# A convolution on one core: the steps that make later weights paced over the images, their loads a set earlier, and GpSimd released by an earlier VectorE step

## Chip, cores and metric

The kernel runs on one core of one Trainium2 chip. The metric is the time of one execution on the device in microseconds (us). Runs of the kernel before took 978.03, 979.94 and 983.44 us; their median, 979.94 us, is the time before.

## What is computed

The input has 160 images of 128 channels and 32 by 32 pixels. They belong to five sets of weights. In the kernel's order, an image has a place from 0 to 159, and 32 in a row use the same set.

```python
xn  = group_norm(x, groups=32)            # groups of 4 channels, eps 1e-5
s1  = (max(U) - min(U)) / 3;  s2 = s1 / 5
v1  = s1 * floor(U / s1);     v2 = s2 * floor((U - v1) / s2)
w   = (v1 + v2).reshape(5 * 128, 128, 3, 3)
out = x + conv3x3(xn, w, padding=1, groups=5)
```

The weights are quantised from `U` in two floors, and the result of the convolution is added to the input.

## The kernel before

**Tiling.** One image is one tile of 128 partitions (channels) by 1024 pixels, and two images make a chunk. The normalised image is held in two parts of 16 bits, a high one (`hi` or `vh`) and a low one (`lo` or `vl`), and TensorE multiplies both by the weights. A 3 by 3 convolution over a pair of lines or columns is done with fewer products than nine: sums and differences of neighbours are multiplied by sums and differences of the weights.

**Two kinds of image.** For some images only the low part goes through the sums (`rows`, made by `low_part` L697 and `combinations` L710 to L719). For the *combined* images (`combined`, from image 7 on every odd one; from image 126 on more than half) the sums are taken of the image itself: GpSimd writes the outer columns (`outer_columns`, L632) and one difference (L662) into `v`, VectorE writes the rest (`combine`, L644 and L651), ScalarE scales it to the high part `vh` (L684), and VectorE makes the low part `vl` (`low_combined`, L690).

**One pass of the loop**, for image i, writes instructions for several images in the order of each engine's queue:

- TensorE: the sums of image i+1 into the banks `m1a` or `m1b` and `m2`, then the main products of image i into its bank pair `eo` (L734, L789).
- VectorE: the low part of image i+2; then `pairs` (L846, L848), which turns the sums of image i+1 into the start of its bank pair `eo`; then `combine` for image i+4.
- GpSimd: the differences of image i+4, or its normalised form `z` (L668), together called `beside_pairs`; then the DMA that adds a finished result to its image in memory (L897). Every eight images also the power -0.5 of the variances (L247).
- ScalarE: the copy of a finished bank pair (L874), the copy `m` of the sums (L837), the high parts, and the two passes that measure image means and squares (L202, L209).
- SP (the queue of loads and stores): the load of a coming chunk (L455), and the store of a finished one (L902). The queue is in order. A load waits until the chunk whose buffer it takes has been stored.

Nothing is scheduled by a planner: the order is the order in which the Python code writes the instructions, and engines wait for one another by semaphores. The one wait added by hand is `after`: GpSimd's differences and its power step wait for the VectorE instruction `last`, the one that stands ahead of `pairs`, so that they run beside `pairs`.

**Weights of the later sets.** While images of set n run, VectorE makes the weights of set n+1: three columns with 14 steps each (L101 to L127, and L507), 42 in all, on tiles of 128 by 384. `load_set` (L448) loads the raw weights into the only buffer of its pool. Each column is transposed by TensorE and kept by ScalarE (L527). Then six more VectorE steps (`sums_of_set`, L531 to L533) make the tables of sums. All steps stand in a generator `later`, from which each pass takes one or more:

```python
if b == (2 if n == 0 else 0):
    self.load_set(n + 1)
if b == (4 if n == 0 else 2):
    later = (s for col in self.COLS for s in self.make_column(n + 1, col))
```

Here b is the image's place in its set. Two steps are taken between one `pairs` and the next: for image i+2 not combined, one between `lo` and `rows` and one ahead of `pairs`; else one right after the preceding `pairs` and one between `vl` and `pairs`. At b of 28 what is left of `later` is written at once.

The statistics of eight images make a group. After the power step, VectorE scales them (`scales_by_vector`, L268 and L270), at the end of the pass, behind `combine`.

Of the kernel before, what the change touches and what calls it, by code (L numbers as in the profile page):

```python
# [16 lines left out]
N_SETS = 5  # L17
# [11 lines left out]


WIDEST = 40.0


class Steps:
# [107 lines left out]
def run(steps):  # L142

    while True:
        try:
            next(steps)
        except StopIteration as end:
            return end.value
# [197 lines left out]
class Main:  # L346
# [308 lines left out]
    def beside_pairs(self, i, after):  # L655
# [14 lines left out]
            )  # L670
        self.after(ins, after)

    def after(self, ins, before):

        self.tc.add_manual_dep(
            ins.ins, before.ins.name,
            mybir.DependencyInfo(mybir.DependencyClass.Sync, mybir.DependencyReason.DATA),
            reason="beside_pairs",
        )
# [226 lines left out]
    def run(self):  # L906
# [49 lines left out]
        def take(steps, count, last=None):  # L956
            for _ in range(count):
                last = next(steps, None) or last
            return last
# [73 lines left out]
        run(self.combinations(3))  # L1033
        self.steps.choose()
        ready, middle, scaled, measured, loaded = [], [], [], self.EARLY, 6
        later, turned = iter(()), []
        for i in range(self.imgs):
            n, b = self.place(i)

# [31 lines left out]
            ahead = i + min(10 + i // 4, self.STAT_LEAD + 1)  # L1071
            to_measure = range(measured, min(self.imgs, ahead))
            measured += len(to_measure)
            if n + 1 < N_SETS:
                if b == (2 if n == 0 else 0):
                    self.load_set(n + 1)
                if b == (4 if n == 0 else 2):
                    later = (s for col in self.COLS for s in self.make_column(n + 1, col))
            by_scalar = [k for k in to_measure if not self.by_vector(k)]
            by_vector = [k for k in to_measure if self.by_vector(k)]  # L1080

            if i < self.FIRST:

                if i == 0:
                    measure(0, 8, 9, 10)
                    self.normalise(4)
                    self.high_part(4)
                if i == 2:
                    self.leave(3)
                    self.normalise(5)  # L1090
                    measure(1, 9)
                    self.high_part(5)
                    self.pairs(3)
                    measure(0, 11)
                    self.low_part(4)
                    run(self.combinations(4))
                self.residual(j)
            else:

                last = None  # L1100
                if self.combined(i + 2):
                    last = last_of(self.low_combined(i + 2))
                elif i + 2 < self.imgs:
                    self.low_part(i + 2)
                    take(later, 1)
                    last = last_of(self.combinations(i + 2))
                last = take(later, 1, last)
                for st in scaled:
                    self.after(st.power(), last)
                if i + 4 < self.imgs:  # L1110
                    self.beside_pairs(i + 4, last)
                if i > self.FIRST and self.by_hand(j):
                    self.residual(j)
                for k in by_scalar:
                    self.measure(k, (0,))
                if i > self.FIRST and not self.by_hand(j):
                    self.residual(j)
                    self.accumulate(j)
                part = i + 3 < self.imgs and not self.combined(i + 3)
                if i + 1 < self.imgs:  # L1120
                    self.leave(i + 1)
                for st in ready:
                    if not st.late:
                        st.deviations()
                if part:
                    if self.by_scalar_too(i + 3):
                        self.normalise(i + 3)
                    self.high_part(i + 3)
                if self.combined(i + 3):
                    self.high_combined(i + 3)  # L1130
                for k in by_scalar:
                    self.measure(k, (1,))
# [8 lines left out]
            for n_of, col in turned:  # L1141
                self.keep_taps(n_of, col)
                if col == self.COLS[-1]:
                    later = self.sums_of_set(n_of)
            turned = []

            if i >= self.FIRST:

                if i + 1 < self.imgs:
                    self.pairs(i + 1)  # L1150
                if self.combined(i + 4):
                    self.combine(i + 4)
                else:
                    take(later, 1)
                if b == self.per_set - 4:
                    run(later)
                for st in ready:
                    if st.late:
                        st.deviations_by_vector()
                for st in scaled:  # L1160
                    st.scales_by_vector()

            scaled, middle, ready = [st for st in middle if st.late], ready, []
            if i >= self.FIRST:
                measure(0, *by_vector)
# [57 lines left out]
```

## Time and profile before

| | us |
|---|---|
| median of 3 runs (lowest to highest) | 979.94 (978.03 to 983.44) |
| the profiled execution, its own time | 982.18 |
| its span | 980.5 |
| TensorE busy (matmuls) | 943.3 |
| VectorE busy | 913.8 |
| ScalarE busy | 833.4 |
| GpSimd busy | 353.5 |

The profile is of one execution. Its lines name the engine (PE is TensorE, PEld its weight loads, DVE is VectorE, ACT is ScalarE, POOL is GpSimd, SPq the queue of SP), the line of the code, the output and the inputs by the program's names without their numbers, and the shapes. In a timeline a line begins with the start and the duration in us; a bracket at its end tells how long the engine sat idle before it and what ended that.

### The profile page before, as it was taken

How to read it: one execution, taken by the hardware profiler on the slowest of the kernel's cores; microseconds unless marked ns; L12 is line 12 of the kernel's file. 1: busy time of each engine (PE TensorE's matmuls, PEld its weight loads, DVE VectorE, ACT ScalarE, POOL GpSimd, SP SyncE). 2: the span in 40 equal slices, each digit the busy share in tenths (PEclk: the TensorE clock that was granted, in tenths of full speed). 3: DMA queues.
4: the chain of work that ended last, by engine and by line, in shares of the span. 5: the costliest groups of instructions: out<-in, count | busy, mean ns of one | idle time of the engine just before them, and what ended most of it. 6: DMA issues, size and time to landing. Idle time of an engine off the chain costs nothing.

```text
span 980.5 us, 13236 instructions
## 1 busy us (share of the span) xinstructions
PE 943.3 (96%) x4504; PEld 440.8 (45%) x4504; DVE 913.8 (93%) x1332; ACT 833.4 (85%) x1135; POOL 353.5 (36%) x441
## 2 busy tenths in 40 slices
PE   2899999999999999999999999999999999999997
PEld 1444444444444444444444444444444444444443
DVE  7999999998999999899999998799999998989995
ACT  5779889999999999889898989698989899898551
POOL 4353333343333333333343333233433434333530
PEclk9999999999999999999999999999999999999999
DMA  9627889999998888999998999998989989998774
GB/s 352 264 95 207 230 236 267 265 250 257 319 297 242 269 232 244 257 289 273 250 267 240 272 247 253 285 281 265 239 261 259 258 249 269 247 247 251 178 207 160
DMA packets 65117, 245.86 MB, mean 251 GB/s; under 512 B 5008, under 2 KB 5008, under 8 KB 65040
## 3 DMA queue, kind: packets, MB, share of 16 engines
q1 hardware_dynamic: 45312, 173.09, 49.4%
q0 software_dynamic: 19728, 71.84, 38.8%
q8 instruction: 37, 0.61, 0.2%
q14 instruction: 40, 0.33, 0.1%
HBM read 89.19 MB, written 83.89 MB: 177 GB/s over the span
## 4 chain that ended last, share of the span: by engine, by line
PE 74%; DVE 12%; DMA 6%; issue 4%; ACT 2%; POOL 2%; SPq 0%; DVEq 0%; POOLq 0%
PE eo L789 25%; PE eo L734 23%; PE m L789 12%; PE m1b L789 8%; PE m1a L789 5%; DMA out_dram<-xt 3%; DVE vl L690 2%; DVE v L644 1%; DMA u<-in_L_conv_U_dram 1%; DVE lo L697 1%; DVE eo L846 1%; DMA xt<-sum 1%; DMA range<-in_L_conv_U_dram 1%; DVE eo L848 1%; DVE v L651 1%
## 5 line engine op out<-in xcount | busy, mean ns | idle before, releaser
L734 PE MATMUL eo<-hi,wt 128*128 128x496 f16 (+2 forms) x1386 | 367.7, 375 | 0.7 <-ACT wt L527 0.7
L789 PEld LDWEIGHTS <-wt 128*128 128x128 f16 x1884 | 183.9, 99 | 216.1 <-DVE rows L719 5.2
L734 PEld LDWEIGHTS <-wt 128*128 128x128 f16 x1458 | 142.6, 99 | 163.7 <-ACT wt L527 1.4
L874 ACT COPY sum<-eo 128x1024 f32<-128x1024 f32 x137 | 143.1, 1045 | 63.2 <-PE eo L789 63.0
L690 DVE SCALAR_TENSOR_TENSOR vl<-v,rstd,vh 128x2048 f16<-128x2048 f32 x82 | 192.2, 2344 | 1.4 <-ACT vh L684 1.4
L789 PE MATMUL eo<-vh,wt 128*128 128x496 f16 (+1 forms) x492 | 185.0, 376 | 1.0 <-DVE eo L848 0.9
L789 PE MATMUL eo<-vl,wt 128*128 128x496 f16 (+1 forms) x492 | 184.9, 376 | 0.0
L684 ACT ACTIVATE vh<-v,rstd 128x2048 f16<-128x2048 f32 x82 | 164.1, 2001 | 17.1 <-DVE v L651 16.9
L209 ACT ACTIVATE junk<-xt,mv 128x1024 f16<-128x1024 f32 x152 | 174.3, 1147 | 0.1
L202 ACT ACTIVATE junk<-xt 128x1024 f16<-128x1024 f32 x152 | 160.6, 1057 | 15.2 <-DMA xt<-in_x_dram 11.6
L789 PE MATMUL eo<-rows,wt 128*128 128x496 f16 (+1 forms) x450 | 170.8, 380 | 0.0
L789 PEld LDWEIGHTS <-across 128*128 128x128 f16 x984 | 96.2, 98 | 116.0 <-issue 5.1
L668 POOL TENSOR_SCALAR z<-xt,ngm,rstd 128x1024 f32<-128x1024 f32 x53 | 62.8, 1184 | 232.3 <-DVE tt L109 39.6
L632 POOL TENSOR_SCALAR v<-xt,ngm 128x64 f32<-128x64 f32 x82 | 30.9, 377 | 257.1 <-issue 72.7
L897 POOL DMA_DIRECT2D xt<-sum x137 | 119.8, 878 | 4.4 <-ACT sum L874 3.1
L837 ACT ACTIVATE m<-m 128x512 f32<-128x512 f32 x157 | 94.0, 599 | 24.9 <-PE m L789 18.7
L644 DVE TENSOR_TENSOR v<-xt 128x960 f32<-128x960 f32 x82 | 106.2, 1295 | 2.8 <-POOL v L632 2.8
L789 PE MATMUL m<-vl,across 128*128 128x496 f16 (+1 forms) x246 | 92.1, 374 | 3.3 <-DVE vl L690 3.2
L697 DVE TENSOR_TENSOR lo<-z,hi 128x1024 f16<-128x1024 f32 x78 | 94.9, 1216 | 0.0
L789 PE MATMUL m<-vh,across 128*128 128x496 f16 (+1 forms) x246 | 92.1, 375 | 0.0
L662 POOL TENSOR_TENSOR v<-xt 128x512 f32<-128x512 f32 x82 | 84.8, 1034 | 0.0
L602 ACT CAST hi<-z 128x1024 f16<-128x1024 f32 x78 | 81.5, 1044 | 1.2 <-POOL z L668 0.5
(144 smaller groups left out, 1151.8 us busy)
## 6 DMA issues: line engine op xcount, KB each, us to landing
xt<-in_x_dram SPq DMA_DIRECT2D x78, 1024.0 KB, 7.0
out_dram<-xt SPq DMA_DIRECT2D x78, 1024.0 KB, 8.7
xt<-sum POOLq DMA_DIRECT2D x137, 512.0 KB, 7.2
u<-in_L_conv_U_dram SPq DMA_DIRECT2D x4, 576.0 KB, 9.7
xt<-in_x_dram SPq DMA_DIRECT2D x4, 512.0 KB, 9.9
range<-in_L_conv_U_dram SPq DMA_DIRECT2D x3, 576.0 KB, 8.1
out_dram<-xt SPq DMA_DIRECT2D x3, 512.0 KB, 2.7
u<-in_L_conv_U_dram SPq DMA_DIRECT2D x2, 288.0 KB, 3.0
```

The lines of the kernel that those rows point to most:

```text
L202: self.nc.scalar.activation(junk, image, ACTF.Copy, scale=-1.0 / image.shape[1], accum_out=self.mv[:, j, 0:1],)
L209: self.nc.scalar.activation(junk, image, ACTF.Square, bias=self.mv[:, j, 0:1], accum_out=self.mv[:, j, 1:2],)
L644: nc.vector.tensor_tensor(self.view(v, 1, (511, 2), (half, H), (1, half - 1)), self.view(x, 1, (1, 2), (W, H), (2, half - 1)), self.view(x ...
L662: ins = nc.gpsimd.tensor_sub(self.v[i][:, 1536:], odd, even)
L684: self.nc.scalar.mul(vh, self.v[i], st.rstd[:, j])
L690: yield self.nc.vector.scalar_tensor_tensor(vl, self.v[i], st.rstd[:, j], self.hi[i], ALU.mult, ALU.subtract)
L697: self.nc.vector.tensor_sub(lo[:, 1 : self.H + 1, :].rearrange("p h w -> p (h w)"), self.z.pop(i), self.hi[i].rearrange("p h w -> p (h w)"),)
L734: nc.tensor.matmul(self.bank(target, a)[:, first:end, c0:c1], self.wts[n, col][:, k, :], tile[:, s0 : s0 + 2 * (end - first) - 1 : 2, c0 + ...
L789: self.nc.tensor.matmul(out, weights, moving, start=start and j == 0, stop=False, skip_group_check=True)
L837: self.nc.scalar.mul(m2, self.m2_ps, 0.5)
L874: nc.scalar.copy(self.as_banks(i, self.sum[i]), self.flat(i, eo))
L897: self.nc.gpsimd.dma_start(self.image(i), self.sum.pop(i), accum_op=ALU.add)
```

## The change

- `load_set(n + 2)` is called at b of 30, two images ahead of the end of a set: at image 30 for set 2, 62 for set 3 and 94 for set 4, instead of 32, 64 and 96. Set 1 is loaded at image 2, as before.
- The steps of a column start at b of 1 instead of 2 (set 0: 4, as before), and a class `Later` hands them out at a pace: an account grows by 42/25 with each image (set 0: 42/22), and each step takes 1 from it. The sums are handed out with a pace of 3 an image. What is left is written at b of 28 and again at b of 30.
- For a combined image i+2, up to two steps are written between `vl` and `pairs`; the step behind the preceding `pairs` is taken only where image i+4 is not combined and the account allows it.
- GpSimd's power step and differences depend on the VectorE instruction ahead of `last` (`last_but_one`).
- `scales_by_vector` is written right behind `pairs`, ahead of `combine`.

`SCALAR` and `take_scalar` of the new class are not used by the program.

```diff
+class Later:
+    def __init__(self, steps=(), pace=0.0):
+        self.steps = iter(steps)
+        self.pace, self.due = pace, 0.0
+        self.scalar = False
+    def next_image(self):
+        self.due += self.pace
+    def take(self, count, last=None):
+        for _ in range(count):
+            if not self.scalar and self.due >= 1.0:
+                step = next(self.steps, None)
+                self.scalar = step is SCALAR
+                if not self.scalar:
+                    last = step or last
+                    self.due -= 1.0
+        return last
...
+    def finish(self):
+        run(self.steps)
...
+    def last_but_one(self, last):
+        of_engine = (
+            i for i in reversed(self.nc.cur_bb.bb.instructions) if i.engine == last.ins.engine
+        )
+        next(of_engine)
+        return next(of_engine)
...
-        later, turned = iter(()), []
+        later, turned = Later(), []
...
+            if i == 2:
+                self.load_set(1)
+            if b == self.per_set - 2 and n + 2 < N_SETS:
+                self.load_set(n + 2)
             if n + 1 < N_SETS:
-                if b == (2 if n == 0 else 0):
-                    self.load_set(n + 1)
-                if b == (4 if n == 0 else 2):
-                    later = (s for col in self.COLS for s in self.make_column(n + 1, col))
+                if b == (4 if n == 0 else 1):
+                    later = Later(
+                        (s for col in self.COLS for s in self.make_column(n + 1, col)),
+                        42 / (self.per_set - 6 - b),
+                    )
+            later.next_image()
...
-                    take(later, 1)
+                    later.take(1)
                     last = last_of(self.combinations(i + 2))
-                last = take(later, 1, last)
-                for st in scaled:
-                    self.after(st.power(), last)
+                last = later.take(2 if self.combined(i + 2) else 1, last)
                 if i + 4 < self.imgs:
-                    self.beside_pairs(i + 4, last)
+                    before = self.last_but_one(last)
+                    for st in scaled:
+                        self.after(st.power(), before)
+                    self.beside_pairs(i + 4, before)
...
-                    later = self.sums_of_set(n_of)
+                    later = Later(self.sums_of_set(n_of), 3.0)
...
                     self.pairs(i + 1)
+                for st in scaled:
+                    st.scales_by_vector()
                 if self.combined(i + 4):
                     self.combine(i + 4)
                 else:
-                    take(later, 1)
-                if b == self.per_set - 4:
-                    run(later)
+                    later.take(1)
+                if b in (self.per_set - 4, self.per_set - 2):
+                    later.finish()
...
-                for st in scaled:
-                    st.scales_by_vector()
```

More of the change, by code (lines that the diff above doesn't have):

```diff
@@ L31, with take_scalar @@
 WIDEST = 40.0
+SCALAR = "the next step is ScalarE's"
+class Later:
[14 more added lines that the diff above has]
+        return last
+    def take_scalar(self):
+        if self.scalar:
+            next(self.steps)
+            self.scalar = False
+    def finish(self):
+        run(self.steps)
 class Steps:
@@ L671, in beside_pairs @@
         self.after(ins, after)
+    def last_but_one(self, last):
[4 more added lines that the diff above has]
+        return next(of_engine)
     def after(self, ins, before):
         self.tc.add_manual_dep(
-            ins.ins, before.ins.name,
+            ins.ins, before.name,
             mybir.DependencyInfo(mybir.DependencyClass.Sync, mybir.DependencyReason.DATA),
```

## Prediction

> **What bounds the kernel now.** I read the page's busy times first, then the stretches of 20 us, then the waits of TensorE, then the timeline where it waits.
>
> ```profile
> PE 943.3 (96%) x4504; PEld 440.8 (45%) x4504; DVE 913.8 (93%) x1332; ACT 833.4 (85%) x1135; POOL 353.5 (36%) x441
> 120.00:140.00 20.00, 18.23 (x88) 8.32 (x87) 19.79 (x35) 18.58 (x26) 4.21 (x5) 1.00 0.87 233
> 140.00:160.00 20.00, 18.01 (x86) 8.00 (x85) 19.54 (x31) 16.26 (x22) 6.35 (x8) 1.00 0.89 246
> 160.00:180.00 20.00, 19.43 (x96) 9.19 (x94) 19.79 (x31) 19.27 (x31) 10.89 (x16) 1.00 1.04 290
> ...
> 620.00:640.00 20.00, 17.80 (x80) 7.76 (x79) 13.95 (x26) 15.80 (x21) 4.20 (x5) 0.91 0.98 319
> ```
>
> The columns are the length, then busy us of PE, PEld, DVE, ACT and POOL, then TensorE's clock. Every stretch from 180 to 960 us but 620:640 shows 19.86 to 20.00 of PE, so TensorE sets the time there, however full VectorE is. PE's idle 37 us lie in the first 80 us (23.3), after 960 (6.7), and in the four rows above (6.5). Only these rows are within the change's reach.
>
> ```profile
> 124.38 0.39 PE L789 MATMUL eo<-vh,wt 128*128 128x512 f16 x1 [0.40 <-DVE eo L848]
> 128.78 0.38 PE L789 MATMUL m<-vl,across 128*128 128x512 f16 x1 [1.34 <-DVE vl L690]
> 148.36 0.82 PE L789 MATMUL m<-rows,wt 128*128 128x512 f16 x3 [0.37 <-DVE rows L719]
> 150.17 0.39 PE L789 MATMUL eo<-vh,wt 128*128 128x512 f16 x1 [0.34 <-DVE eo L848]
> 154.37 0.38 PE L789 MATMUL m<-vl,across 128*128 128x512 f16 x1 [1.27 <-DVE vl L690]
> 178.49 0.38 PE L789 MATMUL m<-vl,across 128*128 128x512 f16 x1 [0.56 <-DVE vl L690]
> ```
>
> Six waits, 4.28 us, all for VectorE, which is 98 to 99% busy in those rows: here VectorE is the bound. The other place is one event.
>
> ```profile
> 614.19 0.46 SPq L448 DMA_DIRECT2D u<-in_L_conv_U_dram  x1
> 626.17 0.47 DVE L101 TENSOR_SCALAR nnn<-u,s1r 128x384 int16<-128x384 f32 x1 [5.95 <-DMA u<-in_L_conv_U_dram]
> 627.98 0.82 PE L789 MATMUL m<-rows,wt 128*128 128x512 f16 x3 [2.01 <-DVE rows L719]
> 629.97 0.61 PE L789 MATMUL eo<-vh,wt 128*128 128x512 f16 x1 [0.19 <-DVE eo L848]
> ```
>
> The first step on the weights of the last set waits 5.95 us for them, VectorE's rows come late behind it, PE idles 2.20 us, and then its matmuls take 0.6 us instead of 0.38: the clock is at half for 3.41 us (mean 0.91 in the row), which costs another 1.7. Together 3.9 us. The other three later sets did not wait for their weights.
>
> **What the skill says.** "SBUF — State Buffer", section "SBUF: two separate sides": VectorE's instructions with two SBUF inputs and GpSimd's instructions exclude each other; whichever starts first keeps the shared port for its whole length. The trace agrees: L644 takes 1.15 us alone, about 1.31 in half of its 82 cases, where L662 of GpSimd still runs, and 1.99 in the five behind a power step.
>
> ```profile
> 140.94 1.03 POOL L247 TENSOR_TENSOR rstd<-ve,mhalf 128x4 f32<-128x4 f32 x1 [2.67 <-DVE tt L110]
> 141.98 0.37 POOL L632 TENSOR_SCALAR v<-xt,ngm 128x64 f32<-128x64 f32 x1
> 142.32 1.03 POOL L662 TENSOR_TENSOR v<-xt 128x512 f32<-128x512 f32 x1
> ...
> 142.39 1.99 DVE L644 TENSOR_TENSOR v<-xt 128x960 f32<-128x960 f32 x1 [0.26 <-POOL v L632]
> ```
>
> "TensorE: Matmul & The Clock Gate", "What's actually happening": after an idle window of about 3.4 us the array's clock is halved until it has been busy for one. Here 2.01 us of idleness sufficed for one window of 3.41 us. "VectorE: DVE Perf Modes", "The DRAIN you can't avoid": a semaphore between consecutive instructions costs nothing extra. The trace differs where the second needs the first's result: in a row, L109 to L112 start 0.65 us apart (35.93, 36.58, 37.24, 37.89), while between other work such a step takes some 0.53 us of VectorE's time. So 0.12 us for each such pair.
>
> **The change part by part.** The sum stands on the profiled execution, 982.18 us (span 980.5, and 1.7 around it), 2.2 above the median of 979.94; without the 3.9 us event it would be 978.3, next to the fastest run (978.03). I therefore take it that the event lies in some runs only. That is a choice, since the runs have no traces.
>
> 1. *Weights in the preceding set.* SP issues in order, and its loads wait for stores to land (69 waits, 568.2 us). Before, the load stood behind the pair at 613.26 and 613.72; the entry ahead of that is the store at 599.90, 13.4 us earlier. Image 30 puts it right behind that store, at some 600.3. With the same 12 us it lands at 612.3. The first step moves one image forward, to about 615.3 (pairs of image 98 start at 615.9). It is 3 us early instead of 6 late. For set 2 it is 227.4 plus 9.7, against a step at 245. Its buffer was last read some eight images earlier, so SP gains no wait. Behind it on SP stand an image load and a store; 576 KB at 250 GB/s delays these by 2.4 us at most. ScalarE would meet that (it waited 1.8 us for an image at 619.75) and has room (18.1 of 20 busy). Gain 3.9 in a run with the event, 0 otherwise.
>
> 2. *Pacing.* 42 steps at 42/22 an image in set 0 (42/25 later) instead of two. In the two programs' order, up to the vl step ahead of the waits at 128.78, 154.37 and 178.49, the changed one has 17, 24 and 32 steps where there were 19, 27 and 35. A step is worth 0.5: 1.0, 1.5 and 1.5 us. One of them is only moved behind the vl step, and GpSimd's start follows it. Against that, both steps of an image with combined parts now stand in a row: three, four and six dependent pairs, 0.4, 0.5 and 0.7 us. Net 0.6, 1.0, 0.8. The eo steps now come 2.5 us after vl (two steps and 1.34); TensorE's twelve products from vl to eo last 2.5 as well, so I add nothing.
>
> 3. *GpSimd one step earlier.* GpSimd starts 0.12 to 0.18 us after the VectorE step that it waits for. Released by the step before, it would stand at the port when the last one ends, and that delay is gone. L644's surplus from 66 us on is 0.09, 0.10, 0.11, 0.17, then 0.84 with a gap of 0.35, 0.15, and 0.84 with 0.35. Small ones vanish (0.5 by 128, 0.6 by 154); a power step saves 0.2 to 0.6, I take 0.4 for each of two. Bounds: 0, if GpSimd isn't ready at the port, and 0.2 us a pair of images. 0.9 by 128, 1.4 by 154, 1.6 by 178.
>
> 4. *Scales ahead of the combination.* L268 and L270 (0.3 us) now stand right behind the eo steps and can wait for the power: at most 1.67 less 1.34, and a landing, 0.45 us, once in eight images. Where the combination follows, VectorE waited there for L632 anyway. I take 0 for the stretch.
>
> 5. *Sums and the rest.* In sets 0 to 2 the sums come some three images later; at the end of set 3 six of 0.35 us now meet the denser combined images from 124 on. In the chain of waits vl takes 2.26 us of VectorE, the two v steps 1.21 and 0.66, the eo steps 1.34, lo 1.13 and rows 1.3: pairs 124 to 126 then need 18.0 us (6.9, 4.8 and 6.3), against the 17.3 between pairs 123 and 126 (766.6 to 783.9). VectorE has a lead there; 0 to 1.5, I take 0.3. Otherwise, between 180 and 960 us, PE is full, so fewer VectorE steps gain nothing.
>
> Waits left in the stretch: by 128, 1.74 less 1.5; by 154, 3.72 less 2.4, so 1.3; by 178, 4.28 less 2.4, so 1.9. Once waited, time is not gained back, so about 1.9 stays: gain 2.4 (1.0 to 4.0). Sum: 982.18 - 3.9 - 2.4 + 0.3 = 976.2.
>
> **The rivals.**
> - *The stretch clears wholly.* Power steps run beside the last step, and vl ahead of its step counts. Then 4.28 is gained: 982.2 - 8.2 = 974.0, a floor. For it: every wait there is VectorE's. Against it: the dependent pairs.
> - *The weights' event is not in the runs, or comes back.* If SP lags, or u lands in 15 us instead of 12, the step waits again: 976.2 + 3.9 = 980.1. With the stretch unchanged as well, 978 to 982.
> - *GpSimd takes the port from vl (slower).* Where no step is left, 23 times, the last VectorE step is vl itself (L690), and GpSimd is released by what stands ahead. If vl then waits for ScalarE by more than GpSimd's 0.15 us, L632 and L662 take the port for 1.42 us, or L668 for 1.18. All 23 times 1.4 is 32 us on VectorE; if a third reaches PE, 976.2 + 11 = 987. Against it: vl waited for vh three times, 1.4 us in all, and the set's ends and set 4 have VectorE at 16 to 19 of 20.
>
> **How the numbers follow.** A run can tell about 0.5% from no change, 4.9 us: faster is below 975.0, slower above 984.8. The likeliest, 976.2 (974.8 to 978), has 0.43, of which a tenth lies below 975.0; the cleared stretch 0.29, nearly all below; the event's return or nothing gained 0.14; the lost port 0.14. Faster 0.33, same 0.53, slower 0.14. The range starts at the floor less the runs' scatter, 973.5, and reaches to 982.5; 0.14 above and a few hundredths below are left out.
>
> **What would show it.** In the changed profile: no wait of L101 for u, and no half clock near 628 us; DVE waits of PE between 118 and 180 us down from 4.28 to about 1.9; L644 nearer 1.15 than its mean of 1.30; POOL's L632 starting within 0.05 us of the end of a VectorE step. Wrong if PE shows new waits past 180 us, if L690 is lengthened past 2.36 us, or if L644 stays at 1.3.

## The result and the profile after

The first four runs of the changed kernel took 992.05, 992.38, 994.58 and 995.92 us; four runs of the kernel before in the same batch took 978.03 to 983.44. The ratio was 1.0128 [1.0088, 1.0169], so these runs were slower by 1.3%, and the prediction, 976.2 us in a range of 973.5 to 982.5, missed. Later runs of the same kernel differ among themselves: of 62 runs on three chips (e5, e12 and f4 below) 24 took 974.5 to 976.7 us, and 28 took 985 to 1002.6. Both have to be explained.

Medians and counts below are over all runs of a kernel; a ratio compares only those runs that lie within 1.5% of the fastest of their kernel.

The profile is of the run of 994.58 us (span 992.9). I call it and its like a late run, since its images come late. First the page: the busy times, and the engines' shares of the chain of work that ended last.

```profile
PE 946.7 (95%) x4504; PEld 439.1 (44%) x4504; DVE 914.3 (92%) x1332; ACT 827.8 (83%) x1135; POOL 418.5 (42%) x441
...
PE 30%; DMA 24%; DVE 22%; issue 10%; ACT 8%; POOL 4%; SPq 0%; DVEq 0%; POOLq 0%; ACTq 0%
```

The same line of the chain in the profile before:

```profile
PE 74%; DVE 12%; DMA 6%; issue 4%; ACT 2%; POOL 2%; SPq 0%; DVEq 0%; POOLq 0%
```

No engine is busy for much longer except GpSimd (353.5 us before), and in the chain DMA has 24% where it had 6%. Next the part that the prediction spoke of, from 118 to 180 us: what TensorE waited for there, the first step on the last set's weights, and one combination behind a power step, all from the timeline.

```profile
123.23 0.39 PE L830 MATMUL eo<-vh,wt 128*128 128x512 f16 x1 [0.21 <-DVE eo L889]
127.16 0.38 PE L830 MATMUL m<-vl,across 128*128 128x512 f16 x1 [0.87 <-DVE vl L731]
136.56 0.39 PE L830 MATMUL eo<-vh,wt 128*128 128x512 f16 x1 [0.21 <-DVE eo L889]
138.91 1.07 POOL L280 TENSOR_TENSOR rstd<-ve,mhalf 128x4 f32<-128x4 f32 x1 [1.84 <-DVE vl L731]
141.50 1.15 DVE L677 TENSOR_TENSOR v<-xt 128x960 f32<-128x960 f32 x1
152.11 0.38 PE L830 MATMUL m<-vl,across 128*128 128x512 f16 x1 [1.01 <-DVE vl L731]
176.06 0.38 PE L830 MATMUL m<-vl,across 128*128 128x512 f16 x1 [0.23 <-DVE vl L731]
...
629.44 0.77 DVE L134 TENSOR_SCALAR nnn<-u,s1r 128x384 int16<-128x384 f32 x1 [0.98 <-DMA u<-in_L_conv_U_dram]
```

The waits are down from 4.28 to 2.53 us. The combination (L677, before it was L644) takes 1.15 us behind a power step, where it took 1.99. The first step on the weights of each of the three later sets waited for them (1.96, 3.06 and 0.98 us): they were asked for earlier, but took 15.5 to 17.4 us to land, where they took 9.4 to 12.0 in the profile before. By 226 us the changed kernel is 2.5 us ahead: the pairs of image 31 start at 226.1 instead of 228.6. All of the loss comes after that. One window of TensorE's busy time with the count of its matmuls shows it; for comparison the same window of the changed kernel in a later, undisturbed run of 975.5 us (e12, span 973.8) follows.

```profile
242.00:694.00 452.00, 439.24 (x2084) 202.07 (x2083) 413.64 (x602) 389.62 (x543) 174.54 (x179) 1.00 0.94 255
```

```profile
242.00:694.00 452.00, 452.00 (x2171) 212.07 (x2170) 434.01 (x628) 409.97 (x564) 180.87 (x186) 1.00 0.95 266
```

The second has 87 matmuls more in the same time; at 452.00 us for 2171 of them that is 18.1 us, of the 19.1 by which the spans differ. (Busy time differs by 12.8 us only; the ends of matmuls are modelled in a profile, so I go by the count.) The waits of the late run name the cause (columns: total us, times, longest).

```profile
ACT junk L235 <- DMA xt<-in_x_dram: 73.2, 29, 7.4
PE m L830 <- ACT m L878: 11.6, 12, 2.1
...
SPq L488 <- DMA out_dram<-xt: 698.5, 69, 15.2
SPq L943 <- DMA xt<-sum: 118.7, 28, 14.7
```

The first and the third of these in the profile before:

```profile
ACT junk L202 <- DMA xt<-in_x_dram: 11.6, 3, 8.1
SPq L455 <- DMA out_dram<-xt: 568.2, 69, 13.6
```

ScalarE waits 29 times for an image that has not arrived, where it waited 3 times. The pass that measures an image (L235) is ahead of the copy `m` (L878) in ScalarE's queue, so the copy comes late, and TensorE, which had never waited for it in the profile before, waits 12 times. The third line is SP: an image load waits until a store has landed.

The timeline shows how the two queues stand to one another in one such place.

```profile
433.40 0.37 SPq L488 DMA_DIRECT2D xt<-in_x_dram  x1
433.87 0.41 SPq L943 DMA_DIRECT2D out_dram<-xt  x1
441.83 1.06 ACT L235 ACTIVATE junk<-xt 128x1024 f16<-128x1024 f32 x1 [6.39 <-DMA xt<-in_x_dram]
444.47 0.81 PE L830 MATMUL m<-rows,wt 128*128 128x512 f16 x3 [2.06 <-ACT m L878]
446.55 0.37 SPq L488 DMA_DIRECT2D xt<-in_x_dram  x1
447.02 0.80 SPq L943 DMA_DIRECT2D out_dram<-xt  x1
```

A load goes out, and 0.47 us behind it a store. The load lands 8.3 us later and ScalarE starts on it at once. The next load has to wait for that store to land, 12.6 us after its issue (446.5), and the next store, long ready, stands behind that load in the in-order queue. So load and store follow each other around a ring: load, store 0.47 us behind it, landing of the store, next load. Between 242 and 694 us the store went out within 0.6 us of the load in 32 of 39 turns. In the profile before it was 12 of 39, and in the undisturbed one 11 of 40; in the others the store follows later. From chunk 24 to chunk 62 the ring turned once in 11.88 us (the loads start at 242.6 and 694.0 us, 38 turns); TensorE needs 11.38 us for a chunk of two images (432.4 us for the same 38 in the profile before). The median landing times from the page's DMA issues close the sum.

```profile
xt<-in_x_dram SPq DMA_DIRECT2D x78, 1024.0 KB, 7.3
out_dram<-xt SPq DMA_DIRECT2D x78, 1024.0 KB, 10.6
...
u<-in_L_conv_U_dram SPq DMA_DIRECT2D x4, 576.0 KB, 16.2
```

The second of these in the profile before:

```profile
out_dram<-xt SPq DMA_DIRECT2D x78, 1024.0 KB, 8.7
```

A store took 10.6 us (median of the run; the means over each 100 us from 200 to 600 lie between 11.0 and 11.7), before 8.7. With 0.47 that is a turn of 11.5 to 12.2 us. Once the images' lead is used up, the ring and not TensorE sets the time. The lead is the time from a load's landing to ScalarE's first use of it. I worked it out from both traces: about 30 us at chunk 6, shrinking in both to 6 to 8 us by chunk 18. Then it was 2.1 and 0.1 us at chunk 23 (before and after); before it recovered to 16 us by chunk 30, after it stayed at 0.1 to 1.8 until chunk 61. In the profile before it came down to 0.1 at chunk 56: that is the load at 613 us, which stands just ahead of the last set's weights in the queue, so that the event of the prediction falls into the same spot. The moved load of the weights is not what used up the lead in the late run: it was down to 1.4 us at chunk 20, whose first use is at 199 us, and the weights of set 2 were asked for at 227.3. In the undisturbed run it was 6.4 us at chunk 20. What makes one run of the same program lose it and another not is not shown.

### The profile page after: what moved, and what is told of

It is laid out like the page before. It is cut to its first block, busy times and chain, and to the rows that moved or that the text cites. A ratio compares the mean times of both kernels' runs of the same rounds, so it can differ in the third digit from the quotient of the medians.

```text
span 992.9 us, 13255 instructions
## 1 busy us (share of the span) xinstructions
PE 946.7 (95%) x4504; PEld 439.1 (44%) x4504; DVE 914.3 (92%) x1332; ACT 827.8 (83%) x1135; POOL 418.5 (42%) x441
## 4 chain that ended last, share of the span: by engine, by line
PE 30%; DMA 24%; DVE 22%; issue 10%; ACT 8%; POOL 4%; SPq 0%; DVEq 0%; POOLq 0%; ACTq 0%
DMA out_dram<-xt 19%; PE eo L830 10%; PE eo L775 9%; PE m L830 5%; DMA xt<-in_x_dram 4%; DVE vl L731 4%; PE m1b L830 3%; DVE v L677 3%; DVE lo L738 3%; ACT vh L725 2%; PE m1a L830 2%; ACT junk L242 2%; DVE eo L887 2%; POOL v L695 2%; DVE eo L889 2%
## 5 line engine op out<-in xcount | busy, mean ns | idle before, releaser
L235 ACT ACTIVATE junk<-xt 128x1024 f16<-128x1024 f32 x152 | 160.6, 1057 | 76.0 <-DMA xt<-in_x_dram 73.2
L731 DVE SCALAR_TENSOR_TENSOR vl<-v,rstd,vh 128x2048 f16<-128x2048 f32 x82 | 194.4, 2371 | 2.9 <-ACT vh L725 2.6
L725 ACT ACTIVATE vh<-v,rstd 128x2048 f16<-128x2048 f32 x82 | 164.0, 1999 | 11.2 <-DVE v L684 10.9
L665 POOL TENSOR_SCALAR v<-xt,ngm 128x64 f32<-128x64 f32 x82 | 72.8, 887 | 237.1 <-issue 64.8
L701 POOL TENSOR_SCALAR z<-xt,ngm,rstd 128x1024 f32<-128x1024 f32 x53 | 85.1, 1606 | 200.4 <-DVE rows L760 107.6
L830 PEld LDWEIGHTS <-across 128*128 128x128 f16 x984 | 96.0, 98 | 127.4 <-issue 18.1
L938 POOL DMA_DIRECT2D xt<-sum x137 | 120.1, 880 | 10.8 <-ACT sum L915 9.7
L878 ACT ACTIVATE m<-m 128x512 f32<-128x512 f32 x157 | 93.7, 597 | 21.4 <-PE m L830 15.3
L677 DVE TENSOR_TENSOR v<-xt 128x960 f32<-128x960 f32 x82 | 94.6, 1153 | 0.0
## 6 DMA issues: line engine op xcount, KB each, us to landing
out_dram<-xt SPq DMA_DIRECT2D x78, 1024.0 KB, 10.6
```

Source lines behind the costliest of these rows:

```text
L235: self.nc.scalar.activation(junk, image, ACTF.Copy, scale=-1.0 / image.shape[1], accum_out=self.mv[:, j, 0:1],)
L677: nc.vector.tensor_tensor(self.view(v, 1, (511, 2), (half, H), (1, half - 1)), self.view(x, 1, (1, 2), (W, H), (2, half - 1)), self.view(x ...
L725: self.nc.scalar.mul(vh, self.v[i], st.rstd[:, j])
L731: yield self.nc.vector.scalar_tensor_tensor(vl, self.v[i], st.rstd[:, j], self.hi[i], ALU.mult, ALU.subtract)
L830: self.nc.tensor.matmul(out, weights, moving, start=start and j == 0, stop=False, skip_group_check=True)
L878: self.nc.scalar.mul(m2, self.m2_ps, 0.5)
```

## The experiments

### First: does a part of the change cause the late images?

Three theories stood against each other. **Q**: the weights' load, moved in the queue, holds up image loads. **P**: the early release of GpSimd does it. **L**: a faster front only brings the kernel sooner to where loads are late. e1, e2 and so on are the runs.

**e1: only the weights' load moved.**

```diff
+            if i == 2:
+                self.load_set(1)
+            if b == self.per_set - 2 and n + 2 < N_SETS:
+                self.load_set(n + 2)
             if n + 1 < N_SETS:
-                if b == (2 if n == 0 else 0):
-                    self.load_set(n + 1)
```

> The kernel before, with only the loads of the later weights moved to the place of the change (image 30 of the preceding set), so that SP issues them ahead of an image load instead of behind a store. Theory Q (SP's in-order queue): the weights delay the image load behind them by some 3 us and the store beside them, the lead of the image loads, 1.6 to 2.1 us before at chunks 23 and 24, is used up, and each further load waits for a store that lands in 11 to 12 us: ScalarE waits for images some 50 to 75 us in all, time 988 to 994. Theory P (GpSimd's earlier release): nothing but the event at 626 us can change, 978 to 981. Theory L (the front of the run is faster, so loads come due earlier): as P, 977 to 982.

20 runs: median 985.71 us (978.14 to 1019.0), ratio 1.0006 [0.9977, 1.0035].

**e2: the change without that** (loads at their old places, columns begun at place 2).

> The changed kernel with the loads at their old places (images 32, 64, 96) and the columns begun at place 2 of a set instead of 1; pacing, order of the scales and GpSimd's release stay. Theory Q: the image loads keep their lead, ScalarE waits under 15 us for images, time 975 to 980. Theory P: still slow, 988 to 994. Theory L: still slow in most part, 985 to 992, since the first 200 us are as fast as in the changed kernel.

12 runs: median 983.56 (975.31 to 997.12), ratio 0.9994 [0.9949, 1.0039].

**e3: the change with GpSimd's release undone.**

```diff
-                    before = self.last_but_one(last)
+                    before = last.ins
```

> The changed kernel with GpSimd's power steps and differences depending on the last VectorE step again, all else as changed. Theory Q: still slow, 987 to 994. Theory P: fast, 976 to 981, and GpSimd's L665 back at 0.38 us. Theory L: in between, the front loses 0.5 to 1 us of its gain and the loads come due that much later: 984 to 992.

20 runs: median 983.17 (976.2 to 995.39), ratio 1.0008 [0.998, 1.0036].

**e4: the kernel before with the release alone.**

```diff
...
-                for st in scaled:
-                    self.after(st.power(), last)
                 if i + 4 < self.imgs:
-                    self.beside_pairs(i + 4, last)
+                    before = self.last_but_one(last)
+                    for st in scaled:
+                        self.after(st.power(), before)
+                    self.beside_pairs(i + 4, before)
```

> The kernel before with only GpSimd's power steps and differences depending on the VectorE step ahead of the last one. Theory Q: no loss, 976 to 981, with L644 at 1.15 us and 0.5 to 1.5 us less waiting of TensorE between 118 and 180 us. Theory P: slow, 986 to 994, with image loads late. Theory L: a small loss where loads come due earlier, 979 to 986.

13 runs: median 979.09 (975.58 to 990.4), ratio 0.996 [0.9931, 0.9989].

None of the three theories was confirmed, because of what the kernel before did in the same batch: 56 runs with a median of 982.04 and a span of 977.36 to 997.5, 16 of them at 985 or above. Every kernel here, with or without any part of the change, has runs some 15 us or more above its best. So no part of the change is needed for a late run. What all these kernels share is the queue of loads and stores, and the comparison needed another question. That the load alone makes late runs more frequent is neither shown nor excluded: e1 had 11 of 20 at 985 or above against 16 of 56 of the kernel before, a difference that chance makes about once in twenty times.

### Second: is it the ring?

Two theories of the ring: **chain** (a load waits for the landing of the store just ahead, and the next store stands behind that load) and **bytes** (the DMA engines have too much to move, and the weights' 576 KB tip them over).

**e5: the changed kernel again**, unchanged, on another chip.

> The changed kernel once more, on the chip of this batch, as the measure for the three that follow. The theory now (chain): SP's queue has load, store, load, store; a load waits for the store ahead of it to land, and the next store stands behind that load, so once the loads have lost their lead each cycle of two images takes the landing of a store, 11 to 12 us and more, against TensorE's 11.6, and nothing wins the lead back. It expects 988 to 996, with ScalarE waiting 50 us or more for images. The rival (bytes): the DMA engines simply have no more room. It expects the same here.

20 runs: median 983.57 (974.58 to 1002.22), ratio 0.9975 [0.9937, 1.0013]; 9 runs lay at 974.6 to 976.7 and 9 at 985 or above, where both theories had expected 988 to 996. The profiled run was one of the quick ones (span 973.2): ScalarE waited three times for an image, 10.9 us, and VectorE never for the later sets' weights.

**e6: the change with no load of weights for sets 2 to 4.** These sets compute with the weights of set 1.

```diff
             if b == self.per_set - 2 and n + 2 < N_SETS:
-                self.load_set(n + 2)
+                self.us[n + 2] = self.us[1]
```

> The changed kernel without the loads of the weights of sets 2, 3 and 4 (1.8 of 245.9 MB; the weights of set 1 are quantised again in their place, so this part of the computation is left out). Chain: what takes the last of the lead at images 30, 62 and 94 is gone, the lead is small but holds for longer, 976 to 984. Bytes: three times 2.4 us less, 985 to 989.

20 runs: median 978.12 (974.85 to 1003.83), ratio 0.9961 [0.9926, 0.9997], 8 of 20 at 985 or above. The profiled run took 990.67 us; one line of its waits:

```profile
ACT junk L235 <- DMA xt<-in_x_dram: 67.7, 32, 7.9
```

The images were late as in the first profile, with no load of weights after the first set's. The weights are not needed for it.

**e7: the change with the store ahead of the load**, two statements swapped:

```diff
+            self.store(i - 2)
             while loaded * NB < min(self.imgs, i + self.LOAD_LEAD):
                 self.load(loaded)
                 loaded += 1
-            self.store(i - 2)
```

> The changed kernel with the store of a pass issued ahead of its load (two statements swapped), so that a load waits for a store that was issued a cycle earlier, and no store stands behind a load that waits. Chain: stores no longer follow one another at the pace of their landing, the lead holds, ScalarE waits under 20 us for images, 974 to 979. Bytes: no gain, 988 to 996, since the same bytes move.

20 runs: median 977.24 (975.97 to 979.55), ratio 0.9928 [0.9904, 0.9952].

**e8: the same swap in the kernel before.**

> The kernel before with the same swap. Chain: the runs of 985 to 997 us, which the kernel before shows too, become rare, and the median falls to 977 to 980. Bytes: median and scatter stay, 980 to 984.

20 runs: median 980.71 (978.89 to 982.03), ratio 0.9984 [0.9959, 1.001].

The scatter is gone in both: 3.6 and 3.1 us from lowest to highest, where the kernel before had 977.15 to 996.84 in the same batch. The bytes are the same, so the theory of bytes falls. The chain theory was right on the scatter and not on the median of e8, for which it had expected 977 to 980. The waits and the DMA issues of e7 show the ring open.

```profile
PE m L830 <- ACT m L878: 1.4, 1, 1.4
...
SPq L943 <- DMA xt<-sum: 758.3, 84, 15.9
SPq L488 <- DMA out_dram<-xt: 32.5, 15, 2.9
```

```profile
xt<-in_x_dram SPq DMA_DIRECT2D x78, 1024.0 KB, 9.8
out_dram<-xt SPq DMA_DIRECT2D x78, 1024.0 KB, 5.8
```

SP now waits in front of a store, for the data of that store (758.3 us), and a load finds its store landed nearly always (32.5 us in 15 waits instead of 698.5 in 69). The store, which goes out first, lands in 5.8 us instead of 10.6; the load takes 9.8 instead of 7.3, and nothing waits for it in a ring. Against the expectation, the lead did not come back: it is under 0.15 us at 29 of the 62 chunks from 18 on, as many as in the late run, and ScalarE waited 29 times for an image (52.2 us, expected under 20). But TensorE waited once for ScalarE's copy, 1.4 us instead of 11.6. So a small lead costs little by itself; it costs much where it leaves the pace of the loads to the ring.

Two reservations. The swap changed two things at once: the next store no longer stands behind a waiting load, and a store lands in 5.8 us. Either could end the late runs (with 5.8 us even a closed ring would turn in 6.3, against TensorE's 11.4), and no run parts the two. And the swap is not free: the best runs of e7 and e8 took 975.97 and 978.89, where the same kernels with the load ahead had 974.58 and 977.15 in the same batch.

### Third: what is each part worth where nothing scatters?

All of these are on the base of e8, the store ahead of the load. The batches ran on different chips; the lowest run of the kernel before was 977.36, 977.15, 977.14 and 977.21 us in the four, so I compare medians across them to some tenths of a microsecond.

**e9: the release alone** (e4's edit).

> The kernel before with store ahead of load, which holds the scatter within 2 us and so shows small differences, and with GpSimd's earlier release alone. The whole change gained 3.5 us on this base (980.71 to 977.24). The prediction's step gives this part 1.6 of its 2.4 us: 979.1. Theory R (the release is nearly all of it): 977.2 to 978.2. Theory S (the pacing is): 980 to 981.

20 runs: median 976.86 (975.4 to 979.12), ratio to the kernel before 0.995 [0.9928, 0.9971]. Against e8 that is a gain of 3.85 us. TensorE's busy time, e8 first, then e9:

```profile
118.00:180.00 62.00, 57.55 (x274) 26.38 (x273) 61.09 (x100) 53.66 (x73) 22.72 (x31) 1.00 0.94 252
180.00:300.00 120.00, 118.58 (x570) 55.39 (x568) 111.36 (x159) 107.04 (x149) 42.16 (x49) 1.00 0.99 278
```

```profile
118.00:180.00 62.00, 58.45 (x280) 26.94 (x279) 61.35 (x100) 53.88 (x74) 24.40 (x31) 1.00 0.95 255
180.00:300.00 120.00, 119.82 (x575) 56.02 (x574) 113.32 (x166) 109.88 (x152) 52.28 (x50) 1.00 0.99 280
```

That is 0.9 us more in the predicted stretch and 1.2 in the one behind it; from 780 to 960 us TensorE has 180.00 instead of 178.51, another 1.5. (The spans of the two profiled runs differ by 5.1.) Behind 180 us the difference is two single waits of e8 that e9 does not have:

```profile
225.90 0.38 PE L789 MATMUL m<-vh,across 128*128 128x512 f16 x1 [1.42 <-ACT m L837]
828.36 0.38 PE L789 MATMUL m<-vl,across 128*128 128x512 f16 x1 [1.35 <-DVE vl L690]
```

The second is a wait for VectorE, like those in the stretch. The first is for ScalarE's copy, and e7, which has the release too, has it as well (1.41 us at 223.78). So that the release removes this one is not shown. The median lies below the range of theory R, and further below that of S.

**e10: the weights' load alone** (e1's edit).

> The kernel before with store ahead of load, and with the loads of the weights two images earlier alone. The prediction gives 3.9 us only to runs that have the event of the first profile, nothing to others: 980.7. If late weights cost a little in every run, 978 to 980; if the earlier weights disturb image loads, 981 to 984.

12 runs: median 980.34 (978.34 to 983.31), ratio 0.9995 [0.9964, 1.0026]. That is 0.4 us from e8, inside the noise, and VectorE waits for no later weights in either profile.

**e11: the pacing alone** (the class `Later` and its calls; loads, scales and release as before, columns begun at place 2, so that the pace of the later sets is 42/24 an image instead of 42/25).

> The kernel before with store ahead of load, and with the pacing of steps and sums alone (columns begun at place 2, loads at their old place, GpSimd released by the last step, scales at the end of the pass). The prediction gives this part 0.8 us: 979.9. Theory R: 980 to 981. Theory S: 977.5 to 979.

10 runs: median 985.75 (984.17 to 987.47), ratio 1.0052 [1.0027, 1.0078]. It costs 5.0 us against e8. In the profile TensorE is no longer full where e8 has 320.00:

```profile
300.00:620.00 320.00, 317.60 (x1518) 147.40 (x1516) 305.45 (x439) 287.13 (x399) 113.29 (x131) 1.00 0.93 257
```

One of its waits in this stretch, from the timeline:

```profile
387.30 0.39 PE L830 MATMUL eo<-vh,wt 128*128 128x512 f16 x1 [0.68 <-DVE eo L889]
```

**e12: the changed kernel a third time.**

> The changed kernel a third time, on the chip of this batch. The first four runs took 992 to 996 us, the twenty of the second time 974.6 to 1002. If it is chance in each run (whether the image loads lose their lead), a third or more of the runs take 974.5 to 977 and some 40% over 985. If it belongs to a chip, nearly all lie together, either at 975 or at 992 and above.

20 runs: median 976.39 (974.51 to 1000.96), ratio 0.9963 [0.9926, 1.0000]; 5 runs at 985 or above. Quick and late runs stand side by side on one chip.

### Fourth: why do the parts not add up?

Release, load and pacing alone give 3.9, 0.4 and -5.0, in sum -0.7, yet the whole change on this base (e7) gained 3.5. Three runs each add one more part to the pacing of e11.

**f1: pacing and release.**

```diff
-                    before = last.ins
+                    before = self.last_but_one(last)
```

> On the base with the store ahead of the load: pacing as in the change, and GpSimd released by the last VectorE step but one; the weights' load and the scales stay where the kernel before has them. Theory R (the pacing loses because it puts up to two later steps ahead of the release, and the release one step earlier takes that back): about 977, like the whole change on this base. Theory S (the scales' place decides): it stays near 985.

22 runs: median 978.73 (975.9 to 981.12), ratio 0.996 [0.994, 0.9981].

**f2: pacing, and the weights' load in the preceding set** with the columns begun at place 1.

> On the base with the store ahead of the load: pacing as in the change and the weights' load in the preceding set, with the columns begun at place 1; GpSimd on the last step, the scales where the kernel before has them. Theory R: it stays at 984 to 987. Theory U (pacing alone loses because the columns wait for weights loaded two images before): about 979 to 981.

14 runs: median 982.76 (980.12 to 985.52), ratio 1.0006 [0.9978, 1.0035].

**f3: pacing, and the scales ahead of the combination.**

> On the base with the store ahead of the load: pacing as in the change and the scales ahead of the combination; the load and GpSimd's release as in the kernel before. Theory R: it stays at 984 to 987. Theory S (behind the paced steps the scales come late, and their images with them): about 979 to 981.

22 runs: median 985.78 (983.44 to 987.93), ratio 1.0036 [1.0013, 1.006].

| on the base with the store ahead of the load | median, us | against e8 |
|---|---|---|
| e8: nothing of the change | 980.71 | |
| e9: release | 976.86 | -3.9 |
| e10: load | 980.34 | -0.4 |
| e11: pacing | 985.75 | +5.0 |
| f3: pacing, scales | 985.78 | +5.1 |
| f2: pacing, load | 982.76 | +2.1 |
| f1: pacing, release | 978.73 | -2.0 |
| e7: all of the change | 977.24 | -3.5 |

The scales' place is worth nothing. The release takes back 7.0 us of the paced kernel's time, against f3 in the same batch and e11 in the one before, nearly twice what it gives by itself; the earlier load with the earlier column start takes back 3.0. Neither theory fits alone: R had expected 984 to 987 of f2, and U 979 to 981, and it took 982.76; R has the larger share. U's own reason, columns that wait for their weights, is small in the traces: VectorE waited 0.9 us for later weights in e11 and 0.4 in f3. f2 also begins the columns one image earlier, and no run tells which of its two parts helps. The pacing is a loss even with the release: 978.73 against 976.86. How the loss comes about is shown only in part. In e11 and in f3 TensorE waits three times between 300 and 620 us for the eo steps, 0.7 us each, at the same three places (340, 387 and 574 us); that is 2.1 us of the 5. There image i+2 is not a combined one, and VectorE has a paced step (0.55 us) and the addition of a finished result (L932, 1.21 us) ahead of the eo steps. With the release (f1) one of the three is left, 0.35 us. In e11's profile three smaller waits for VectorE behind 300 us add 1.1 us, and 1.6 us are lost before 56 us, where TensorE's clock fell to half near 40 us; in f3's it did not. On the other side e11 lacks the wait of 1.42 us at 226. The combination, 1.28 us on the mean in e8, takes 1.32 in e11 and 1.26 in f3, with the same time for both, so a longer hold of the port does not explain it. The rest stays open.

**f4: the changed kernel a fourth time.**

> The changed kernel as it is, on the chip of this batch. If the lost lead of the image loads comes run by run, as in the two batches before: lowest run 974 to 976, a third of the runs at 985 or above, the median between 976 and 984. If some chips hold it in the late state: nearly all runs at 990 to 996, as in the first four.

22 runs: median 986.4 (975.24 to 1002.59), ratio 0.9997 [0.9965, 1.0029]; 14 at 985 or above, 7 at 990 or above, with the quick runs among them. That is more late runs than the third that was expected, and a higher median. Still they come run by run on this chip as on the two before, so no chip was found that makes all runs late.

## Why the prediction was wrong, and where it was right

**The step that failed is the bound itself.** The prediction read from 20 us rows of one execution that TensorE sets the time from 180 us on, that "only these rows are within the change's reach", and in step 1 that the load and store behind the weights' load would be delayed by 2.4 us at most, which ScalarE "has room" for. The prediction's own sign of being wrong, new waits of TensorE past 180 us, is what came: 12 waits for ScalarE's copy, 11.6 us. In the execution that the prediction read TensorE was full, but the images reached ScalarE with a lead of only 0.1 to 3 us in 18 of the chunks from 23 on. The number that points at it stood in step 1, 568.2 us of SP's waits for stores, and was used only to place the weights' load. Followed one link further it is a ring of 0.47 us plus a store's landing against 11.4 us of TensorE's work: at the 8.7 us median of that profile it has room, at 11.0 to 11.7 it has none. e7 and e8 show that this ring is the cause of the late runs: with two statements swapped, none of 40 runs reached 985 us. (They do not tell whether the opened ring or the store's faster landing did it.) Step 1 also reckoned with a landing of 9.7 to 12 us for the weights; in the late run they took 15.5 to 17.4.

**The second failure is the scatter.** Three runs from 978 to 983 were taken for the spread of the kernel before. In the batches of e5, e12 and f4 it had 191 runs with a median of 982.6, of which 68 lay at 985 or above. The upper end of the range, 982.5, would have had to be near 1000 for a single run. The rival "the weights' event comes back" came true and was, as I read it, the small visible end of this: the weights late at 626 us stood behind a load and a store of the ring, and in e8, with their load at its old place, no later weights were waited for. The price, 3.9 us, was that of one late load, not of a ring that stays closed for 450 us.

**The sum held for an undisturbed run, though not by its terms.** 24 of 62 runs took 974.5 to 976.7, and 976.2 lies among them. In the quick profile of e5 it even falls in the two places of the prediction: against the profile before, the pairs of image 31 start 2.6 us earlier (2.4 predicted for the stretch), and the span is 7.3 us shorter, most of the rest coming near 620 us, where the profile before waits for weights and this one does not (3.9 predicted). That is in part luck, for the parts by themselves do not give it. Term by term, on the base that doesn't scatter:

- *Weights in the preceding set*, predicted 3.9 in runs with the event and 0 otherwise: 0.4 alone (e10), which is nothing, as forecast for runs without the event; in the undisturbed profiles of e5 and e12 the later steps don't wait for weights. 3.0 in the company of the pacing (f2), together with the columns' start, which was not foreseen.
- *Pacing*, predicted to gain 0.8: it costs 5.0 alone and 1.9 beside the release. In the stretch the sign was right: TensorE's waits there are 4.3 us in e8, 3.1 with the pacing (e11), 3.6 with the release (e9) and 2.6 with both (f1). On the whole it was wrong. The step put the later place of the eo steps at nothing, 2.5 us against 2.5, and what the pacing does past 180 us too, since TensorE was full there in one profile; in e11 TensorE waits for the eo steps three times, 0.7 us each.
- *Release*, predicted 1.6: 3.9 alone. The mechanism was right: L677 is at 1.15 to 1.18 us in all 82 cases, and GpSimd's L665 rose from 0.38 to 0.89 us on the mean, which I read as the time that it now waits at the port. The size was wrong because the gain was counted to 180 us only, and TensorE was not full behind that: in e9 only 0.9 us lies in the stretch, less than the 1.6, and waits of 1.42 and 1.35 us behind it are gone, the first of them perhaps not by the release.
- *Scales*, predicted 0: 0.0 (f3 against e11).
- *Sums of the set*, 0.3: not tried by themselves.
- *The stretch*, 1.9 us of waits left: 2.53 in the first profile, 2.5 (62.00 less 59.50 busy) in that of e12.
- *The lost port*, the rival on the slower side: vl (L731) was lengthened twice of 82, to 3.49 and 3.34 us, and three times in the quick profile of e12. It did not decide. The slower runs came from a resource that no rival named.

**What stays open.** All four of the first runs were late, at 992 us or more; of the 62 later ones 12 were. At that rate four in a row come by chance once in some 700 times, so something of that batch is not understood. Whether the changed kernel falls into the ring more often than the one before is not settled either. 19 of 62 runs (31%) lay 13 us or more above its lowest (974.5), and 29 of 191 (15%) of the kernel before above its own (977.1); if each run is independent, chance makes such a difference once in a hundred times. Counted from 985 us for both it is 28 of 62 against 68 of 191, which chance makes easily. A kernel that is faster by 2.6 us when undisturbed has less time for a turn of the ring, which would fit, but no run tests this.

**A version without late runs** that is faster than the kernel before is that kernel with the store ahead of the load and the release alone, e9: 976.86 us, ratio 0.995 [0.9928, 0.9971], and no run above 979.12. The changed kernel had a median of 976.39 in the same batch (e12) and quicker best runs, but a quarter of its runs at 985 or above.

## What to carry to other kernels

Where a load waits for a store and the next store stands behind that load in the same queue, work out the turn of the ring, issue to issue plus the landing, and hold it against the compute time of a turn; read each load's lead and not only whether someone waits for it. A small lead is a warning and not a loss: it was as small in e7, a run of 977.3 us, as in the late run of 994.58, where the ring set the pace. Here it helped to issue first the transfer on whose landing the queue itself waits. Parts of a change to an engine's order are not to be added up: measured by themselves and together they differed by 4 us here, so the sum of a prediction needs its range from the pairs that can help or hurt one another.

## What the runs showed of the hardware

- Of two transfers of 1 MB issued close together, the order decides which is slow: load ahead of store, 7.3 and 10.6 us to landing (first profile of the change); store ahead of load, 5.8 for the store and 9.8 for the load (e7). These are medians over the whole run; of the pairs within 0.6 us alone they are 6.7 and 10.8, and 5.5 and 9.2.
- A gap in TensorE's work does not by its length alone decide whether the clock drops. Near 39 us, after 1.59 us of waiting, twelve matmuls took 2.87 us at full clock in e7; in e11, after 1.20 us at the same place, the same twelve took 4.61. What the traces show instead is how the idle time falls into windows of 3.41 us. In all 18 traces a spell of full or of half clock is a whole number of these long (e11: 13.65 us full, 3.41 half, 935.25 full), but for the last one, which the end of the kernel cuts off. Here are the windows of e11, then of e7, around that place; TensorE's busy time is the number behind the comma, and its clock the third from the end.

```profile
37.11:40.53 3.42, 1.64 (x13) 0.75 (x11) 3.18 (x7) 0.82 (x2) 0.25 (x1) 1.00 0.00 0
40.53:43.94 3.41, 3.41 (x10) 1.26 (x9) 3.17 (x6) 3.38 (x5) 1.47 (x3) 0.50 0.02 5
```

```profile
35.83:39.24 3.41, 1.79 (x13) 0.79 (x10) 3.20 (x6) 0.00 (x0) 0.00 (x0) 1.00 0.11 37
39.24:42.65 3.41, 2.86 (x14) 1.39 (x15) 3.17 (x6) 3.37 (x5) 1.72 (x3) 1.00 0.02 5
```

In e11 the waits of 1.20 and 0.58 us lie in one window, which has 1.78 us of idle time, and the next window is at half clock. In e7 they are longer together, but the edge of a window parts them, 1.62 and 0.55 us. Up to the end of its work, TensorE's clock fell to half behind windows with 1.78 to 3.08 us of idle time (seven times in six traces, among them the 2.01 us of the prediction) and behind none with 1.77 or less. One window with 1.83 us, in e3, did not bring it, so the border lies near 1.8 us here, as far as the modelled ends of the matmuls let it be read.
